# First 3x3 convolution filtered along rows and columns, its chunks in turns with the second's

## The chip, the cores and the metric

The kernel is one program on one core of a Trainium2 chip. The metric is the device time of one execution in microseconds; lower is better. Everything is float32.

## The reference, cut to what matters

The input x has shape (4, 256, 56, 56). Four layers follow each other, each of the form x = x + layer(groupnorm(x)): an involution, a block of two 3x3 convolutions, a second involution, and a channel and spatial gate. The change touches the second layer alone:

```
def layer1(x, w1, g1, b1, rm1, rv1, w2, g2, b2, rm2, rv2):
    h = relu(bn(conv3x3(x, w1), g1, b1, rm1, rv1))     # 256 -> 256 channels, padding 1
    h = bn(conv3x3(h, w2), g2, b2, rm2, rv2)
    return relu(x + h)

x = x + layer1(groupnorm(x), ...)                      # 32 groups of 8 channels
```

bn in evaluation mode is a scale and a shift for each channel. Group norm is folded into a scale `rstd` and a shift for each channel, from statistics that the layer before gathers.

## The kernel before

TensorE is called PE here, VectorE DVE, ScalarE ACT, GpSimd POOL. Channels lie on the 128 partitions, in NB = 2 blocks of 128. `conv_layer` runs between two calls of `involution_layer`, and each of the three opens its own memory pools, so that the next stage's tiles can be written only when the last users of the old ones are done. Images pass between stages through DRAM.

**Filtering along rows.** Both convolutions use the minimal filtering algorithm F(4,3) along image rows: four output columns come from six products instead of twelve. A row of 56 columns is cut into WT = 14 tiles of four. `input1` splits a normalised chunk of rows on ACT into four phases (column modulo 4, tile `ph1`, L937), and `transform` combines the phases on DVE into the six inputs `v[:, k]` (twelve instructions, L905 to L916). `weights` makes six transformed weights `u` from three taps, also on DVE (L871 to L876), after three DMAs for each input block from the ACT queue (L866 to L868). `products` does, for each of two output blocks `co` and each position k, six matmuls that add up in one PSUM bank: two input blocks and three row taps dy, the tap being a shift by whole rows in `v` (L962). One bank holds up to 20 rows x 14 tiles = 280 columns. ACT and DVE then read the six banks and combine them to four output phases (L974 to L985).

**Chunks.** The first convolution's rows are cut as C1_ROWS = (0, 20), (20, 38), (38, 56), the second's as C2_ROWS = (0, 16), (16, 36), (36, 56). For each of the four images the three chunks of the first convolution run, then the three of the second. `conv1` writes its outputs by ACT into `ph2` (L994), which holds the whole image in phases; `conv2` reads the residual input from DRAM, normalises it on ACT (L1011), adds the products (L1017), rectifies and adds in one DVE instruction (L1020), takes statistics (L1023) and stores by a DMA from the POOL queue (L1024). The transform of the next chunk is written ahead of the products of the current one, so that PE does not wait for it. The program order in this layer is left to the scheduler.

**PSUM.** Six banks are for products (`mm`), two for the small matmuls of the group norm (`gn`). In a group-norm step a mean over each group of 8 channels is a matmul with `gavg_sb` (L188, L199).

**Other lines that the prediction names.** In the involutions, L408 is a matmul of a bottleneck whose last piece has 112 columns; L498 is a DVE instruction that reads PSUM and an SBUF tile; L503 is a two-input POOL addition; L505 is a DVE instruction with two SBUF inputs; L651 is one of the two-input POOL operations of the gate.

Of the kernel before, what the change touches and what calls it, by code (L numbers as in the profile page):

```python
# [16 lines left out]
P = 128  # L17
# [54 lines left out]
def net_kernel(  # L72
# [762 lines left out]

    def conv_layer(xin, xout):
        with ExitStack() as es:
            wpool = es.enter_context(tc.tile_pool(name="cw", bufs=1))
            work = es.enter_context(tc.tile_pool(name="cwork", bufs=2))
            mm_ps = es.enter_context(tc.tile_pool(name="cmm_ps", bufs=6, space=PSUM))  # L840
            gn_ps = es.enter_context(tc.tile_pool(name="cgn_ps", bufs=2, space=PSUM))

            def one_bank():
                return gn_ps.tile([P, 512], F32, name="gn")


            xb_of = {}

            def load(b):
                xb_of[b] = work.tile([P, NB, HW], F32, name="xb", bufs=1)  # L850
                y0 = 0
                for _, y1 in C1_ROWS:
                    y1 = min(H, y1 + 1)
                    for cb in range(NB):
                        nc.sync.dma_start(xb_of[b][:, cb, y0 * W : y1 * W], xin[b][cb][:, y0 * W : y1 * W])
                    y0 = y1


            u_sb = [wpool.tile([P, NB, 3, WPOS, C], F32, name=f"u{i}_sb") for i in range(2)]

            def weights(i):
                u, wc = u_sb[i], (wc1, wc2)[i]
                for ci in range(NB):
                    w = wc[ci * P : (ci + 1) * P].rearrange("c (y x) n -> c y x n", y=3)
                    w1 = work.tile([P, 3, C], F32, name="w1")
                    nc.scalar.dma_start(u[:, ci, :, 0, :], w[:, :, 0, :])  # L866
                    nc.scalar.dma_start(u[:, ci, :, 5, :], w[:, :, 2, :])
                    nc.scalar.dma_start(w1, w[:, :, 1, :])  # L868
                    w0, w2 = u[:, ci, :, 0, :], u[:, ci, :, 5, :]
                    u1, u2, u3, u4 = (u[:, ci, :, k, :] for k in range(1, 5))  # L870
                    nc.vector.tensor_tensor(u2, w0, w2, ALU.add)  # L871
                    nc.vector.tensor_tensor(u1, u2, w1, ALU.add)  # L872
                    nc.vector.tensor_tensor(u2, u2, w1, ALU.subtract)
                    nc.vector.scalar_tensor_tensor(u4, w2, 4.0, w0, ALU.mult, ALU.add)
                    nc.vector.scalar_tensor_tensor(u3, w1, 2.0, u4, ALU.mult, ALU.add)
                    nc.vector.scalar_tensor_tensor(u4, w1, -2.0, u4, ALU.mult, ALU.add)  # L876
# [12 lines left out]
            norm_of = {}  # L889

            def norm(b):
                rstd, shift = norms[1][b]

                shift2 = small.tile([P, NB], F32, name="shift2")
                nc.vector.tensor_add(shift2, shift, bn["t2"])
                norm_of[b] = rstd, shift, shift2

            def transform(v, ci, ph, n):

                d = [ph[:, j, :, :WT] for j in range(4)] + [ph[:, j, :, 1:] for j in range(2)]  # L900
                vs = [v[:, k, ci, : n * WT].rearrange("p (r t) -> p r t", t=WT) for k in range(WPOS)]
                tmp = [work.tile([P, CV_ROWS + 2, WT], F32, name=f"d{k}", bufs=1) for k in range(3)]
                a, c, e = (t[:, :n] for t in tmp)
                tt, stt = nc.vector.tensor_tensor, nc.vector.scalar_tensor_tensor
                stt(a, d[2], -4.0, d[4], ALU.mult, ALU.add)  # L905
                stt(c, d[1], -4.0, d[3], ALU.mult, ALU.add)
                tt(vs[1], a, c, ALU.add)
                tt(vs[2], a, c, ALU.subtract)
                tt(c, d[4], d[2], ALU.subtract)
                tt(e, d[3], d[1], ALU.subtract)  # L910
# [120 lines left out]
            for b in range(B):  # L1031
                for i in range(3):
                    nv = input1(b, i + 1) if i < 2 else None
                    if i == 2:
                        nv = input2(0)
# [87 lines left out]
```

## Time and profile before

| | us |
|---|---|
| median of 3 runs | 1947.86 |
| lowest and highest | 1942.15, 1957.1 |
| the profiled execution, its own time | 1955.35 |
| span of its profile | 1953.6 |
| first involution, up to its last matmul's follow-up | 0 to 539 |
| convolution matmuls, first start to last end | 555.6 to 1323.2 |
| second involution and gate | 1323.2 to 1953.6 |

The slices of the page show the three stages (each digit is the busy share of a slice of 48.8 us in tenths):

```
PE   5899999999869999999999999997999899999876
DVE  4685767856678686668657865854766666666773
ACT  2345445444343122312331232113655555555532
POOL 2233432334300000000000000000000581580672
```

The profile names an instruction by its line of the kernel, its engine, its operation and the tiles it writes and reads. In a group of instructions the numbers after the bar are the busy time in us, the mean ns of one, and the idle time before them. A matmul's recorded length includes its way through the array, so neighbours overlap; the pace of a row of them is the busy time over the count. The same holds, less strongly, for DVE, whose next instruction starts some 0.08 us before the recorded end of the last if it does not need its result.

### The profile page before, as it was taken

The numbers are of one execution on the slowest core, as the hardware profiler recorded it, in microseconds if no ns is written. First come the engines' busy times: TensorE is split into PE (matmuls) and PEld (weight loads), VectorE is DVE, ScalarE is ACT, GpSimd is POOL, SyncE is SP. The second block draws the span as 40 slices with busy tenths as digits, with TensorE's granted clock in tenths as the row PEclk, the third lists the DMA queues.
The fourth block names the chain that finished last, engine by engine and source line by source line (L and its number), as shares of the span: only waits on it lengthen the run. The fifth ranks groups of instructions, "written<-read, shape, count | busy, mean of one in ns | idle before, by whom it ended". The sixth has DMA issues, their size and how long they took to land.

```text
span 1953.6 us, 55107 instructions
## 1 busy us (share of the span) xinstructions
PE 1801.3 (92%) x23766; PEld 1555.4 (80%) x23766; DVE 1322.8 (68%) x2843; ACT 766.1 (39%) x1672; POOL 433.1 (22%) x631
## 2 busy tenths in 40 slices
PE   5899999999869999999999999997999899999876
PEld 4888879878748987898789888984887777877765
DVE  4685767856678686668657865854766666666773
ACT  2345445444343122312331232113655555555532
POOL 2233432334300000000000000000000581580672
PEclk9999999999979999999999999998999999999995
DMA  3444534444251011101111110113533763763651
GB/s 100 149 148 150 165 107 137 150 130 146 88 206 66 22 67 45 67 32 56 45 67 43 57 34 1 43 47 128 161 130 128 222 175 135 222 188 103 180 151 72
DMA packets 66962, 213.19 MB, mean 109 GB/s; under 512 B 13660, under 2 KB 21648, under 8 KB 63392
## 3 DMA queue, kind: packets, MB, share of 16 engines
q1 hardware_dynamic: 44526, 137.45, 22.5%
q0 software_dynamic: 14848, 65.85, 10.3%
q10 hardware_dynamic: 7346, 6.38, 1.1%
q8 instruction: 187, 3.06, 0.7%
q14 instruction: 55, 0.45, 0.1%
HBM read 73.76 MB, written 49.16 MB: 63 GB/s over the span
## 4 chain that ended last, share of the span: by engine, by line
PE 75%; DVE 13%; DMA 5%; POOL 3%; issue 2%; ACT 1%; SPq 0%; ACTq 0%; POOLq 0%; DVEq 0%
PE mm L962 39%; PE ps L478 16%; DVE kt L454 9%; PE ps L436 8%; PE ps L408 5%; PE ps L364 4%; DVE un L498 1%; PE ps L665 1%; DMA xw<-xw 1%; DMA gx<-x 1%; PE ps L561 1%; DMA w<-in_wc_dram 1%; DMA xs<-in_x_dram 1%; DVE st L807 0%; POOL norm_sb L130 0%
## 5 line engine op out<-in xcount | busy, mean ns | idle before, releaser
L962 PE MATMUL mm<-v,u_sb 128*128 128x280 f32 (+2 forms) x3456 | 766.7, 384 | 19.4 <-DVE u_sb L872 19.4
L962 PEld LDWEIGHTS mm<-v,u_sb 128*128 128x128 f32 x3456 | 653.9, 190 | 126.9 <-issue 19.4
L478 PE MATMUL ps<-kt,xw 126*32 126x48 f32 (+1 forms) x12544 | 382.8, 236 | 46.6 <-issue 23.8
L478 PEld LDWEIGHTS ps<-kt,xw 126*32 126x32 f32 (+1 forms) x12544 | 341.5, 122 | 97.9 <-issue 56.3
L454 DVE TENSOR_TENSOR kt<-ps,zb_sb 126x798 f32<-126x798 f32 x384 | 357.6, 979 | 57.6 <-PE ps L436 56.8
L436 PE MATMUL ps<-hp,z_sb 64*126 64x133 f32 x6144 | 384.1, 280 | 11.0 <-DVE kt L454 6.4
L436 PEld LDWEIGHTS ps<-hp,z_sb 64*126 64x126 f32 x6144 | 366.3, 187 | 25.8 <-DVE kt L454 7.7
L447 ACT ACTIVATE kt<-ps,zb_sb 126x133 f32<-126x133 f32 x768 | 224.6, 442 | 167.5 <-PE ps L436 167.5
L498 DVE SCALAR_TENSOR_TENSOR un<-ps,s,un 128x240 f32<-128x240 f32 x224 | 102.5, 457 | 130.4 <-ACT un L493 126.4
L498 DVE SCALAR_TENSOR_TENSOR un<-ps,par_sb,un 128x240 f32<-128x240 f32 x224 | 98.5, 457 | 122.1 <-ACT un L491 117.9
L1024 POOL DMA_DIRECT2D x<-xr x24 | 13.1, 548 | 560.7 <-DVE xr L1020 515.1
L503 POOL TENSOR_TENSOR xs<-un,xs 128x240 f32<-128x240 f32 x112 | 72.3, 666 | 224.1 <-DVE un L498 224.1
L365 ACT COPY xw<-ps 126x896 f32<-126x896 f32 x112 | 101.6, 907 | 51.0 <-PE ps L364 43.6
L364 PE MATMUL ps<-ident_sb,strip_sb 128*126 128x128 f32 x784 | 112.9, 285 | 2.2 <-ACT un L493 1.3
L408 PE MATMUL ps<-xs,redn 128*128 128x504 f32 (+1 forms) x224 | 98.0, 585 | 9.4 <-DMA xs<-x 7.4
L937 ACT ACTIVATE ph<-xb,norm_sb 128x294 f32<-128x294 f32 (+2 forms) x96 | 80.7, 897 | 64.4 <-DVE d L913 35.9
L493 ACT ACTIVATE un<-ps,bn_t,s 128x240 f32<-128x240 f32 x112 | 60.3, 539 | 116.3 <-PE ps L478 108.5
L491 ACT ACTIVATE un<-ps,par_sb 128x240 f32<-128x240 f32 x112 | 50.3, 449 | 130.3 <-PE ps L478 128.5
L994 ACT ACTIVATE ph<-y,bn_t,bn_s 128x252 f32<-128x252 f32 (+1 forms) x96 | 54.8, 600 | 109.2 <-DVE y L984 73.9
L364 PEld LDWEIGHTS ps<-ident_sb,strip_sb 128*126 128x126 f32 x784 | 85.8, 143 | 11.8 <-ACT un L493 1.4
L130 POOL TENSOR_TENSOR norm_sb<-norm_sb,mhalf 128x1 f32<-128x1 f32 x32 | 18.9, 589 | 338.0 <-DVE norm_sb L129 331.5
L978 DVE SCALAR_TENSOR_TENSOR y<-mm,y 128x280 f32<-128x280 f32 (+2 forms) x48 | 20.5, 427 | 103.2 <-PE mm L962 103.2
(144 smaller groups left out, 1583.3 us busy)
## 6 DMA issues: line engine op xcount, KB each, us to landing
xw<-xw SPq DMA_DIRECT2D x168, 252.0 KB
xw<-xw SPq DMA_DIRECT2D x224, 126.0 KB
xw<-xw POOLq DMA_DIRECT2D x56, 252.0 KB, 4.5
x<-xs POOLq DMA_DIRECT2D x8, 1568.0 KB, 7.7
xs<-in_x_dram SPq DMA_DIRECT2D x6, 1568.0 KB
xs<-x SPq DMA_DIRECT2D x6, 1568.0 KB
x<-xs SPq DMA_DIRECT2D x6, 1568.0 KB
gx<-x POOLq DMA_DIRECT2D x42, 224.0 KB, 5.4
```

Source lines behind the costliest of these rows:

```text
L364: nc.tensor.transpose(ps[:Q, k * P : (k + 1) * P], flat[:, k * Q : (k + 1) * Q], ident_sb)
L365: nc.scalar.copy(xw[:, :NSB, :], ps[:Q, : NSB * P].rearrange("q (n c) -> q n c", n=NSB))
L408: nc.tensor.matmul(ps[:, : rows * W], redn[:, ci].rearrange("p i r -> p (i r)"), xs_of[b, ci][:, j * ROWS_H * W : (j * ROWS_H + rows) * W] ...
L436: nc.tensor.matmul(ps[:Q, i, k * NT : (k + 1) * NT], z_sb[i * R : (i + 1) * R, cb * GB // 2 + gp, z0 : z0 + Q], hp[i * R : (i + 1) * R, py ...
L447: nc.scalar.activation(kt[:, g0 + i, pb, :, k], ps[:Q, i, k * NT : (k + 1) * NT], AF.Identity, bias=zb_sb[:, cb * GB + g0 + i, p0 + k : p0 ...
L454: nc.vector.tensor_tensor(kt[:, g0 : g0 + 2, pb], ps[:Q, :, : PB * NT].rearrange("q i (k t) -> q i t k", k=PB), zb_sb[:, cb * GB + g0 : cb ...
L478: nc.tensor.matmul(v[m * j : m * j + m, i, :, k * TP : (k + 1) * TP], xw[:, window(ty), m * j : m * j + m], kt[:, ng * j : ng * j + ng, :, ...
L493: nc.scalar.activation(part, o[0], AF.Identity, bias=bn["t4"][:, cb : cb + 1], scale=bn["s4"][ng][:, 0, cb : cb + 1])
L498: nc.vector.scalar_tensor_tensor(part, o[e], s, part, ALU.mult, ALU.add)
L503: nc.gpsimd.tensor_tensor(dst, u, dst, ALU.add)
L937: nc.scalar.activation(ph1[:, q, r0 : r0 + hi - lo, t0 : t0 + WT], xr[:, j], AF.Identity, bias=shift[:, ci : ci + 1], scale=rstd[:, ci : c ...
L962: nc.tensor.matmul(ps[:, : n * WT], u[:, ci, dy, k, co * P : (co + 1) * P], v[:, k, ci, dy * WT : (dy + n) * WT], start=(i == 0), stop=(i ...
```

## The change

The first convolution is filtered along both directions: F(4,3) along rows as before and F(2,3) along columns of the image. Two output rows then come from four products over a pair of rows instead of six row taps. The second convolution stays filtered along rows only. Around it the whole layer is written anew:

- `u1_sb` has four row entries y in place of three. `row_weights` makes the row filtering of the weights in steps; `column_weights` then sums them over the taps, for two positions k at a time, on POOL for positions (1, 2) and (0, 5) and on DVE for (3, 4). The factors 1/2 of F(2,3) are in the combination, and part of the factors of F(4,3) goes into the scales (`s1_6`, `scales`).
- `columns` builds the four column inputs of one position from `v` by four POOL instructions of 280 or 252 elements, in two tiles `v2` (five buffers). Positions 1 and 2 are built in the step before, the others inside the step.
- `conv1` does, for each position k, four groups of four matmuls (two output blocks side by side in a bank, two input blocks added), each over half of the chunk's rows: 140 or 126 columns. It reads four banks for each position: one ACT copy, two DVE additions, and two DVE instructions that finish the row pair. A chunk's outputs are combined over both blocks at once, in instructions of 560 or 504 elements, three of them on POOL. Their last part is a `tail` that runs in the next step.
- `conv2` combines its banks as they come. The residual is added before the rectification, scaled so that ACT's scale by `rstd` brings it back; ACT rectifies into `res`, and POOL adds `res` to the input and stores it (`finish`).
- In `transform` the first differences for positions 0 and 5 go to POOL, two of twelve instructions.
- The chunks run in the order conv1(0), conv1(1), conv2(0), conv1(2), conv2(1) and so on over all images, ending with conv2(11). Loads are by chunk and block, with one or two rows read twice.
- All eight PSUM banks form one pool.
- Into each step's twelve places `after[0..11]` the pieces of other chunks' work are put by lists written by hand, and `in_order` then pins every engine to the program order in the layer, from the first matmuls on.

The diff, cut to its core:

```diff
-            mm_ps = es.enter_context(tc.tile_pool(name="cmm_ps", bufs=6, space=PSUM))
-            gn_ps = es.enter_context(tc.tile_pool(name="cgn_ps", bufs=2, space=PSUM))
+            mm_ps = es.enter_context(tc.tile_pool(name="cmm_ps", bufs=8, space=PSUM))
...
+            tt, stt = nc.vector.tensor_tensor, nc.vector.scalar_tensor_tensor
+            ptt = nc.gpsimd.tensor_tensor
...
+            def column_weights(ci, ks, eng, scratch):
+                at = slice(ks[0], ks[1] + 1, ks[1] - ks[0])
+                w0, w1, w2, w3_ = (u1_sb[:, ci, y, at, :] for y in range(4))
+                s = y_tile(scratch)[:, : 2 * C].rearrange("p (k n) -> p k n", k=2)
+                eng.tensor_tensor(s, w0, w2, ALU.add)
+                eng.tensor_tensor(w3_, s, w1, ALU.subtract)
+                eng.tensor_tensor(w1, s, w1, ALU.add)
...
             def transform(v, ci, ph, n):
...
+                ptt(vs[0], d[0], d[2], ALU.subtract)
+                ptt(vs[5], d[5], d[3], ALU.subtract)
...
-                tt(a, d[0], d[2], ALU.subtract)
-                stt(vs[0], c, 0.25, a, ALU.mult, ALU.add)
-                tt(a, d[5], d[3], ALU.subtract)
-                stt(vs[5], e, -4.0, a, ALU.mult, ALU.add)
+                stt(vs[0], c, 0.25, vs[0], ALU.mult, ALU.add)
+                stt(vs[5], e, -4.0, vs[5], ALU.mult, ALU.add)
...
+            def columns(i, k):
...
+                for pair in (((1, 2, ALU.add), (2, 1, ALU.subtract)), ((0, 2, ALU.subtract), (1, 3, ALU.subtract))):
+                    t = work.tile([P, 2 * NB, CV_ROWS // 2 * WT], F32, name="v2", bufs=5)
+                    v2_of.setdefault((i, k), []).append(t)
+                    for e, (p, q, op) in enumerate(pair):
+                        o = t[:, e * NB : (e + 1) * NB, : m * WT].rearrange("p c (r t) -> p c r t", t=WT)
+                        ptt(o, d[p], d[q], op)
+
+            KS = (1, 2, 3, 4, 0, 5)
...
+            def conv1(i, after, tail):
...
+                for s, k in enumerate(KS):
+                    (va, vb) = v2_of[i, k]
+                    banks = []
+                    for v2, e, y in ((va, 0, 1), (va, 1, 3), (vb, 0, 0), (vb, 1, 2)):
+                        ps = one_bank()
+                        banks.append(ps[:, : NB * m])
+                        for co in range(NB):
+                            for ci in range(NB):
+                                nc.tensor.matmul(
+                                    ps[:, co * m : (co + 1) * m],
+                                    u1_sb[:, ci, y, k, co * P : (co + 1) * P],
+                                    v2[:, e * NB + ci, :m],
+                                    start=(ci == 0),
+                                    stop=(ci == NB - 1),
+                                )
+                    m1, m2, m0, m3 = banks
+                    h = work.tile([P, NB * CV_ROWS // 2 * WT], F32, name="h")[:, : NB * m]
+                    nc.scalar.copy(h, m1)
...
+                    tt(o[:, 0], by_row_(h), by_row_(m2), ALU.add)
+                    tt(h, h, m2, ALU.subtract)
+                    run_all(after[2 * s])
+                    stt(o[:, 0], o[:, 0], 0.5, by_row_(m0), ALU.mult, ALU.add)
+                    stt(o[:, 1], by_row_(h), 0.5, by_row_(m3), ALU.mult, ALU.subtract)
+                    if s + 2 < WPOS:
+                        columns(i, KS[s + 2])
+                    if s == 1:
+                        ptt(a, mi[1], mi[2], ALU.add)
+                    if s == 2:
+                        tt(mi[1], mi[2], mi[1], ALU.subtract)
+                    if s == 3:
+                        ptt(b, mi[3], mi[4], ALU.add)
+                    if s == 4:
+                        tt(mi[3], mi[3], mi[4], ALU.subtract)
+                        stt(mi[0], a, -1.0 / 6, mi[0], ALU.mult, ALU.add)
+                        stt(mi[0], b, 1.0 / 24, mi[0], ALU.mult, ALU.add)
+                        ptt(b, b, a, ALU.subtract)
+                    run_all(after[2 * s + 1])
...
+            def conv2(i, after, sums, tail):
...
+                    def residual(y, j, x=xj, co=co):
+                        s = sc[:, 2 if j in (1, 2) else 1, co : co + 1]
+                        y = y.rearrange("p (r t) -> p r t", t=WT)
+                        stt(y, y, s, x[:, j], ALU.mult, ALU.add)
...
+                        else:
+                            yd = part("yd", co)
+                            stt(yd, q, 1.0 / 6, ps, ALU.mult, ALU.add)
+                            stt(yd, t, 1.0 / 3, yd, ALU.mult, ALU.add)
+                            residual(yd, 3)
+                            rectified(yd, 3)
+                            stt(t, t, 0.5, q, ALU.mult, ALU.add)
+                            residual(t, 1)
+                            rectified(t, 1)
+                        run_all(after[WPOS * co + s])
+
+                    def finish(x=x, res=res, co=co):
+                        ptt(x, x, res, ALU.add)
+                        nc.gpsimd.dma_start(xout[bb][co][:, y0 * W : y1 * W], x)
...
+            order = [(1, 0)]
+            for i in range(1, n_chunks):
+                order += [(1, i), (2, i - 1)]
+            order.append((2, n_chunks - 1))
...
+                if conv == 1:
+                    run_all(tail1)
+                    if tail2:
+                        after[0].append(tail2.pop(0))
+                    if nxt is not None and nxt[0] == 2:
+                        j = nxt[1]
+                        place(after, input2(j, 0), (0, 0, 0, 1, 1, 2, 2, 3, 3, 4, 4))
+                        place(after, input2(j, 1), (4, 5, 5, 5, 6, 6, 7, 7, 8, 8, 9))
...
+                    if nxt is not None and nxt[0] == 1:
+                        j = nxt[1]
+                        place(after, input1(j, 0), (1, 2, 2, 2, 3, 3, 3, 3, 3, 4, 4))
+                        place(after, phases(j, 1), (4, 4, 5, 5, 5))
...
+                        place(after, input1(j, 1), (6, 6, 6, 7, 7, 7, 8, 8, 8, 9, 9))
+                        for k in range(2):
+                            after[9 + k].append(lambda j=j, k=k: columns(j, KS[k]))
...
+            in_order(since)
```

In the changed kernel the matmuls of `conv1` are line 1043 and those of `conv2` line 1138, the column inputs line 1019, and the four DVE drains of a position lines 1055 to 1059.

## The prediction

> **What bounds the kernel now.** I read the page's engine row and slices, the chain that ended last, the busy times of the convolution stage, and then the instruction groups by shape.
>
> ```profile
> PE 1801.3 (92%) x23766; PEld 1555.4 (80%) x23766; DVE 1322.8 (68%) x2843; ACT 766.1 (39%) x1672; POOL 433.1 (22%) x631
> ```
>
> ```profile
> 555.60:1323.20 767.60, 767.60 (x3480) 656.91 (x3481) 548.66 (x1340) 195.47 (x308) 19.20 (x44) 1.00 0.14 49
> ```
>
> ```profile
> 555.59 192.83 PE mm L962 x864
> ```
>
> The first line is the page's engine row. The second is the stretch from the first to the last convolution matmul; its columns are length, then busy time of PE, PEld, DVE, ACT, POOL, then the granted clock. PE is busy in all 767.6 us; DVE in 548.7 (71%), POOL in 19. The third line is the chain: one image is a single run of L962 without a wait. So this stage is bound by PE, and what shortens PE shortens it, until another engine takes over.
>
> ```profile
> L962 PE MATMUL mm<-v,u_sb 128*128 128x280 f32 x1728 | 413.6, 400 | 19.4 <-DVE u_sb L872 19.4
> L962 PE MATMUL mm<-v,u_sb 128*128 128x252 f32 x1152 | 245.5, 375 | 0.0
> L408 PE MATMUL ps<-xs,redn 128*128 128x112 f32 x32 | 4.8, 271 | 0.0
> ```
>
> ```profile
> L651 POOL TENSOR_TENSOR gn<-gn,sfb 128x448 f32<-128x448 f32 x42 | 48.7, 1159 | 0.0
> L503 POOL TENSOR_TENSOR xs<-un,xs 128x240 f32<-128x240 f32 x56 | 39.2, 700 | 223.3 <-DVE un L498 223.3
> ```
>
> Busy time over count gives the pace of a matmul record: 0.239 us at 280 columns, 0.213 at 252. A float32 matmul leaves two records (3456 for 1728 in the code). The L408 line has 8 runs of 4 records, each with new weights: (4.8/8 - 0.271)/3 = 0.110 us a record. The POOL lines give 2.2 ns per element and 0.17 us per instruction for two inputs.
>
> ```profile
> 551.78 0.47 DVE L905 SCALAR_TENSOR_TENSOR d<-ph 128x308 f32<-128x308 f32 x1
> 552.17 0.47 DVE L906 SCALAR_TENSOR_TENSOR d<-ph 128x308 f32<-128x308 f32 x1
> ```
>
> ```profile
> 1318.31 0.45 DVE L979 SCALAR_TENSOR_TENSOR y<-mm,y 128x280 f32<-128x280 f32 x1
> 1318.79 0.45 DVE L982 SCALAR_TENSOR_TENSOR y<-y,y 128x280 f32<-128x280 f32 x1
> ```
>
> ```profile
> 1521.43 1.14 POOL L651 TENSOR_TENSOR gn<-gn,sfb 128x448 f32<-128x448 f32 x1
> ```
>
> ```profile
> 1521.86 0.97 DVE L505 SCALAR_TENSOR_TENSOR xs<-un,xs 128x240 f32<-128x240 f32 x1
> ```
>
> From the starts: an independent DVE instruction takes 0.39 us at 308 elements (1.04 ns each plus 0.07); one that needs its predecessor takes 0.48 at 280, so 0.12 more. The last two lines: POOL reads SBUF until 1522.57; DVE L505, which has two SBUF inputs and is 0.41 long in its median, starts inside that time and ends at 1522.83, one plain pass of 240 elements after POOL.
>
> **What the Trainium skill says.** "SBUF — State Buffer", section Who interferes with whom: a DVE instruction with two SBUF inputs and a GpSimd instruction that reads SBUF exclude each other for their whole length; one with at most one SBUF input is left alone. The trace agrees: L505 above, while L498 (PSUM and SBUF inputs) shows 0.47 beside the same POOL work. "TensorE: Matmul & The Clock Gate", section LDWEIGHTS, makes a weight load as long as its columns, 128/1.2 = 107 ns; the 0.110 us at 112 columns fits. "GPSIMD Engine Reference", section 3.1, puts a two-input elementwise operation at about 2.6 cycles per element; 2.2 ns here.
>
> **The change, part by part.**
>
> *PE.* A first-convolution chunk now has 6 x 4 x 2 x 2 = 96 matmuls of half its rows where it had 144/2 = 72 of all rows. Before: 576 records x 0.239 + 1152 x 0.213 = 383 us. After: 768 records at 140 columns and 1536 at 126. The column slope, (0.239 - 0.213)/28, brings 140 columns to about 0.118; at 126 the slope gives 0.10, but the weight load holds it at 0.110. Sum 91 + 169 = 260. PE's need falls by 123 us to 645. Bounds on a record at 126: 0.10 and, were the recorded load length of 0.19 the pace, 0.19.
>
> *DVE, own time* (12 chunks of each convolution, elements from the shapes): first-convolution drains, 288 instructions, 75.3k elements, 133 dependent: 78 + 20 + 16 = 114. Combinations of 504 or 560 elements, 84: 59. Second convolution from PSUM, 144: 56; from SBUF, 96: 39. Residuals, 96, one input with stride 4: 45 if the stride is free, 71 if it costs what L1017 (strided in and out, 0.64 at 280) costs; I take 57. Input transforms, 480 (ten a piece; two went to POOL): 188. Statistics 112 x 0.30 = 34. Norms and the second filter's weights 21. Sum 568 us; two instructions moved to POOL and the saved finishing pass pay for most of what the column sums add. 568 is under PE's 645, but 88% of it.
>
> *POOL.* 288 column instructions x 0.75 = 216; 96 transform parts x 0.80 = 77; 36 combinations x 1.32 = 48; 24 finishing adds x 2.47 = 59; 24 DMA issues x 0.55 = 13. Sum 413 us, from 19. Of it 2.2 ns x 146.6k elements = 322 us hold the read port.
>
> *The port.* 756 DVE instructions (transforms, combinations, residuals, SBUF sums) have two SBUF inputs: 253 us. 322 + 253 = 575, so the port is taken 89% of PE's 645 us. No trace of before shows this mix. Bounds on the DVE time lost: nothing, if POOL always falls on drains from PSUM; 322 us, as DVE works in order and each POOL hold stops at most one of its instructions. Mean hold 0.73 us. About six in ten DVE instructions have two SBUF inputs, so right behind one the next waits the whole hold with chance 0.6 (0.44 us), and behind a PSUM drain POOL's hold is over or nearly so; I take 0.39 us per POOL instruction where DVE is pressed, less a quarter for the time in which DVE waits for PE anyway: 0.29 x 444 = 130 us. DVE then needs 568 + 130 = 698, over PE's 645: it becomes the bound. Add 22 us in which it cannot work (the first drain, half of the last second-convolution chunk of 34 us): stage 720.
>
> *Order.* In a first-convolution step POOL has 16 column instructions, 4 transform parts, 3 combinations and the finishing add: about 22 us for PE's 21 to 23. The finishing add heads POOL's queue there: it waits for the last five DVE instructions and a rectification (2.9 + 0.7 us after the matmuls), holds the queue 3 us, and only behind it come the columns of the third position, wanted 7.2 us in. Worked through, the columns land near 10 us and again late at the fifth position: PE waits some 5 us per step, which is not added, since DVE, not PE, sets the pace then. In the second-convolution steps PE's 27 to 34 us cover all else.
>
> *Ends.* First matmul: before, it waited for weights (DMA to 554.3, DVE 0.97). Now, after the DMAs, POOL has in its queue 5 filter sums for positions 0 and 5 and 6 for positions 1 and 2 (512 elements, 1.3 us each), four transform parts of 0.85 and two columns of 0.8: 19 us from about 549, plus some 5 of port waits against 12 DVE weight sums, so near 573 for 555.6: +17 (bounds +10, +25). Last chunk: the finishing add on POOL (2.5) and a rectification (0.65) stand where DVE's L1020 (1.3) stood: +3. The loads on SP and ACT keep their size but for rows read twice; at a DMA share of 14% they cost nothing.
>
> Sum: 720 + 17 + 3 - 767.6 = -28 us on the profiled 1955.35: 1927. That execution stands 0.4% above the median 1947.86, so 1920.
>
> **The rivals.**
> 1. PE stays the bound: the holds fall on drains, DVE loses under 77 us. DVE has 645 - 568 = 77 us of room. For it: 432 DVE drains from PSUM and 112 statistics, 204 us, can lie beside POOL's holds. Against: transforms and columns are laid in the same steps. 645 + 20 - 767.6 = -103: 1845.
> 2. Slower: DVE and POOL stop each other nearly every time. In the first-convolution steps both have over 21 us of own work for PE's 22, and transforms come in runs of two or three, each waiting a whole column hold. It decides from 0.40 us per POOL instruction (178 us lost: 568 + 178 + 22 = 768; with the ends it is slower already from 0.36). At 0.5: 222 + 568 + 22 + 20 = 832, +64: 2010. Against: the drains between, and POOL's own waits, which give DVE the port.
> 3. The matmuls don't shrink as said: a weight load paces a record at its recorded 0.19 us. 2304 x 0.19 = 438, PE 823, + 20: +75, about 2020. Against: L408's 0.110.
>
> **How the numbers follow.** A run of a kernel like this tells about 1% from no change. Forecast 0.48 (1900 to 1945 for 0.24 to 0.35 us a POOL instruction), rival 1 0.12, rival 2 0.34, rival 3 0.06. Faster by over 1% (under 1928): rival 1 and two thirds of the forecast, 0.45. Within 1%: the rest of the forecast and the near edge of rival 2, 0.20. Slower 0.35. The range 1860 to 2015 leaves out the outer parts of rivals 1 and 2 and rival 3. Both signs hold much of the chance; the forecast's own range is 1900 to 1945.
>
> **What would show it.** In the profile after: L1043 records at 0.11 to 0.12 us in a run; DVE busy above 90% of the stage and its two-input instructions lengthened beside POOL while the drains L1055 to L1059 are not; PE idle in first-convolution steps, released by POOL's L1019 or by DVE; first matmul near 573. I am wrong if PE is busy throughout, if the transforms keep their 0.47 us, or if the stage is over 768 us.

## The result, and the profile after

The changed kernel takes 2060.0 us (median of 4 runs, 2057.7 to 2062.9) against 1946.2 for the kernel before in the same measurement: ratio 1.0576, interval 1.053 to 1.0622. It is slower by 5.8%. The profiled execution took 2057.68 us, its span 2055.9. These are the lines that answer to those shown of before: the page's engine row, the stretch from the first to the last convolution matmul, and the groups.

```profile
PE 1737.3 (85%) x24342; PEld 1532.9 (75%) x24342; DVE 1592.5 (77%) x2890; ACT 814.8 (40%) x1768; POOL 868.1 (42%) x1071
```

```profile
574.60:1437.20 862.60, 708.56 (x4056) 638.04 (x4056) 789.25 (x1363) 236.51 (x395) 427.07 (x468) 0.91 0.13 44
```

```profile
L1043 PE MATMUL mm<-v,u_sb 128*128 128x126 f32 (+1 forms) x2304 | 314.0, 301 | 164.5 <-POOL v L1019 125.3
...
L1019 POOL TENSOR_TENSOR v<-v 128x252 f32<-128x252 f32 (+1 forms) x288 | 219.3, 794 | 0.2
...
L1183 POOL TENSOR_TENSOR xr<-xr,res 128x1120 f32<-128x1120 f32 (+1 forms) x24 | 57.5, 2398 | 128.9 <-ACT res L1125 128.9
...
L973 DVE TENSOR_TENSOR v<-d,d 128x308 f32<-128x308 f32 (+2 forms) x48 | 106.8, 2224 | 0.8
```

PE's work did fall, but the stage went from 767.6 to 862.6 us. PE is idle 154 us of it, DVE is busy in 789 of 863, and the granted clock is 0.91 where it was 1.00. The last line is the one to stop at: L973 adds two tiles of 308 elements, which takes 0.47 us alone, and its mean is 2.22 us. Where before had one unbroken run of L962 in the chain of work that ended last, the chain is now mostly DVE's; these pieces of it (start, length, what) stand around one step from the second convolution to the first:

```profile
752.97 0.40 DVE v L975
753.39 5.99 DVE d L977
759.38 0.40 DVE d L979
...
770.84 0.45 DVE h L1056
771.34 1.63 issue
...
774.15 6.92 DVE v L973
```

Outside the stage: the first matmul starts 19 us later (574.6 for 555.6), and what follows the last matmul is 11.7 us shorter (618.7 for 630.4). Together with the stage's 95 that is the 102 us between the two profiled executions. The medians lie 114 us apart.

### Two kinds of waits

The timeline of the changed kernel at the first of the two long pieces, DVE and POOL:

```profile
752.93 0.56 POOL L1184 DMA_DIRECT2D x<-xr  x1 [0.30 <-POOL xr L1183]
753.39 5.99 DVE L977 TENSOR_TENSOR d<-ph 128x308 f32<-128x308 f32 x1
```

```profile
773.01 0.57 POOL L1184 DMA_DIRECT2D x<-xr  x1 [0.30 <-POOL xr L1183]
773.60 0.86 POOL L964 TENSOR_TENSOR v<-ph 128x308 f32<-128x308 f32 x1
774.07 7.00 DVE L973 TENSOR_TENSOR v<-d,d 128x308 f32<-128x308 f32 x1
774.41 0.85 POOL L965 TENSOR_TENSOR v<-ph 128x308 f32<-128x308 f32 x1
775.22 5.52 POOL L1019 TENSOR_TENSOR v<-v 128x280 f32<-128x280 f32 x8
775.92 10.45 PE L1043 MATMUL mm<-v,u_sb 128*128 128x140 f32 x64 [7.29 <-POOL v L1019]
```

The second one is L973: it stands through ten POOL instructions in a row (two transform parts, eight columns) and ends when the burst ends. There are 17 such stops in the stage, seven of L977 over eight POOL instructions and ten of L973 over ten, 5.6 to 7.0 us each. A DMA issue on POOL, the store of `finish`, ends half a microsecond or less before each of them. The stage has 23 such issues. All 17 with POOL work ready behind them have a long stop, and the six with nothing behind them for 3 us or more have none. Where no DMA issue stands ahead, the engines take turns. Some 13 us later in the same step:

```profile
787.23 7.23 POOL L1019 TENSOR_TENSOR v<-v 128x280 f32<-128x280 f32 x8
787.52 0.93 DVE L987 SCALAR_TENSOR_TENSOR v<-d,v 128x308 f32<-128x308 f32 x1
...
789.09 1.25 DVE L1065 TENSOR_TENSOR y<-y,y 128x560 f32<-128x560 f32 x1
...
790.26 1.07 DVE L969 SCALAR_TENSOR_TENSOR d<-ph 128x308 f32<-128x308 f32 x1
791.25 0.94 DVE L971 SCALAR_TENSOR_TENSOR d<-ph 128x308 f32<-128x308 f32 x1
```

Eight columns of the same size take 7.23 us instead of 5.52, and each two-input DVE instruction waits for about one of them. From here on "lost time" is DVE's time above what the shortest twentieth of the same line and shape takes, summed over the instructions of 200 elements or more in the stage: 219 us here, of which 126 in waits over 1.2 us. The drains L1055 (one SBUF input, the other in PSUM) show no loss: 0.41 us at 252 elements with POOL beside them all the time (31 of them) and without (17).

The page "SBUF — State Buffer" of the Trainium skill, section SBUF: two separate sides, says that of a DVE instruction with two SBUF inputs and a POOL instruction that reads SBUF, whichever starts first has the shared ports for the whole instruction and the other is blocked. The last timeline agrees: each wait is about one POOL instruction. A stop over ten of them, as in the second timeline, goes further than the hold of one instruction, and the experiments look for what brings it. The prediction's "left alone" is narrower on that page (section Who interferes with whom): it holds outside the two-port modes of VectorE. The drains above, at 0.41 us with POOL and without, are left alone.

### The profile page after: what moved, and what is told of

Read it like the earlier page. It is cut to its first block, busy times and chain, and to the rows that moved or that the text cites. A ratio compares the mean times of both kernels' runs of the same rounds, so it can differ in the third digit from the quotient of the medians.

```text
span 2055.9 us, 57328 instructions
## 1 busy us (share of the span) xinstructions
PE 1737.3 (85%) x24342; PEld 1532.9 (75%) x24342; DVE 1592.5 (77%) x2890; ACT 814.8 (40%) x1768; POOL 868.1 (42%) x1071
## 4 chain that ended last, share of the span: by engine, by line
DVE 45%; PE 37%; issue 7%; DMA 4%; POOL 3%; ACT 3%; SPq 1%; ACTq 0%; POOLq 0%; DVEq 0%
PE ps L478 14%; DVE kt L454 9%; PE ps L436 8%; PE ps L408 4%; DVE v L973 4%; PE mm L1138 4%; PE ps L364 4%; DVE y L1122 3%; DVE d L977 3%; DVE d L971 2%; DVE h L1056 1%; DVE un L498 1%; DVE v L983 1%; DVE y L1055 1%; DVE st L1189 1%
## 5 line engine op out<-in xcount | busy, mean ns | idle before, releaser
L1043 PE MATMUL mm<-v,u_sb 128*128 128x126 f32 (+1 forms) x2304 | 314.0, 301 | 164.5 <-POOL v L1019 125.3
L1043 PEld LDWEIGHTS mm<-v,u_sb 128*128 128x128 f32 x2304 | 302.7, 211 | 176.1 <-POOL v L1019 142.0
L1138 PE MATMUL mm<-v,u_sb 128*128 128x280 f32 (+1 forms) x1728 | 396.0, 390 | 7.2 <-DVE u_sb L876 7.2
L1138 PEld LDWEIGHTS mm<-v,u_sb 128*128 128x128 f32 x1728 | 332.6, 194 | 63.4 <-issue 5.4
L1019 POOL TENSOR_TENSOR v<-v 128x252 f32<-128x252 f32 (+1 forms) x288 | 219.3, 794 | 0.2
L1125 ACT ACTIVATE res<-y,cscale,norm_sb 128x280 f32<-128x280 f32 (+1 forms) x96 | 82.5, 859 | 252.0 <-DVE y L1122 251.0
L1052 ACT COPY h<-mm 128x252 f32<-128x252 f32 (+1 forms) x72 | 26.3, 380 | 240.2 <-PE mm L1043 137.6
L964 POOL TENSOR_TENSOR v<-ph 128x308 f32<-128x308 f32 (+2 forms) x48 | 45.6, 949 | 174.5 <-ACT ph L951 170.7
L1183 POOL TENSOR_TENSOR xr<-xr,res 128x1120 f32<-128x1120 f32 (+1 forms) x24 | 57.5, 2398 | 128.9 <-ACT res L1125 128.9
L973 DVE TENSOR_TENSOR v<-d,d 128x308 f32<-128x308 f32 (+2 forms) x48 | 106.8, 2224 | 0.8
```

The source lines that it names most:

```text
L1019: ptt(o, d[p], d[q], op)
L1043: nc.tensor.matmul(ps[:, co * m : (co + 1) * m], u1_sb[:, ci, y, k, co * P : (co + 1) * P], v2[:, e * NB + ci, :m], start=(ci == 0), stop= ...
L1125: nc.scalar.activation(rj[:, j], y.rearrange("p (r t) -> p r t", t=WT), AF.Relu, bias=sc[:, 0, co : co + 1], scale=rstd[:, co : co + 1],)
L1138: nc.tensor.matmul(ps, u2_sb[:, ci, dy, k, co * P : (co + 1) * P], v[:, k, ci, dy * WT : dy * WT + m], start=(j == 0), stop=(j == NB * 3 - 1),
```

## The experiments

A burst is a row of POOL instructions with no pause between them. A slot is one of a step's twelve places `after[0..11]`. Theory A: the DMA issue on POOL lets the burst behind it through without DVE getting a turn. Theory B: taking turns at the port costs this much whatever stands on the queue. Theory C: POOL's order, columns behind `finish`, makes PE wait. Theory D: DVE's own work sets the pace. The ratio to before is given with its interval. Where an expectation speaks of 384 column instructions, it should say 288 (6 positions, 4 instructions, 12 chunks), and its 192 and 256 of them are 144 and 192. The runs lie on several chips, each measured beside the kernel before, so close kernels are compared by their ratios.

| kernel | us | ratio to before | stage | DVE busy (lost) |
|---|---|---|---|---|
| changed | 2060.0 | 1.0576 (1.053-1.0622) | 862.6 | 789 (219) |
| e1 store on SP | 2005.2 | 1.0278 (1.0254-1.0303) | 810.4 | 735 (161) |
| e3 finish in slot 3 | 2061.8 | 1.0576 (1.0548-1.0603) | 866.7 | 792 (224) |
| e2 columns on DVE | 2040.0 | 1.0466 (1.0434-1.0498) | 842.1 | 757 (106) |
| e4 no columns | 1924.4 | 0.987 (0.9834-0.9906) | 736.6 | 663 (103) |
| e5 small DMAs | 2069.4 | 1.0603 (1.0583-1.0623) | 869.9 | 794 (217) |
| e6 store later on POOL | 2027.8 | 1.0397 (1.0371-1.0423) | 829.9 | 753 (183) |
| e7 e1 and e3 | 2011.9 | 1.0309 (1.0287-1.0332) | 818.4 | 736 (174) |
| e8 three banks | 2014.1 | 1.0332 (1.0305-1.0358) | 819.9 | 687 (160) |
| e9 half the columns on DVE | 2007.7 | 1.0298 (1.0235-1.0361) | 816.5 | 708 (157) |
| e10 columns as copies | 1954.7 | 1.0001 (0.9976-1.0026) | 761.9 | 678 (113) |
| e11 rows only | 1975.2 | 1.0108 (1.0063-1.0154) | 794.3 | 560 (102) |
| e12 first two filtered | 1961.6 | 1.0049 (1.0029-1.0069) | 766.2 | 615 (126) |
| e14 last two filtered | 1929.8 | 0.9891 (0.9864-0.9919) | 743.9 | 617 (124) |
| e15 last four filtered | 1945.1 | 0.9964 (0.9944-0.9985) | 763.0 | 695 (155) |

### e1: the store on another queue

```
-                        nc.gpsimd.dma_start(xout[bb][co][:, y0 * W : y1 * W], x)
+                        nc.sync.dma_start(xout[bb][co][:, y0 * W : y1 * W], x)
```

> The store of the residual chunk is issued from SP's queue in place of GpSimd's; nothing else changes. Theory A (the long stops of VectorE, 17 of 5.6 to 7.0 us in the trace of the changed kernel, come from the DMA issue that stands on GpSimd just before its burst of column instructions): these 17 stops shrink to one GpSimd instruction each, under 1.2 us; VectorE's lost time falls from 219 us to some 120, and the time from 2060 to 1950-1990. Theory B (VectorE and GpSimd exclude each other whatever stands on the queue): the long stops stay behind GpSimd's addition, 2030-2060. Theory C (GpSimd's own order, the columns behind the addition): no change but the 0.57 us of each issue, 2040-2060.

All 17 long stops are gone; no DVE instruction waits for more than two POOL instructions. A mere pause of POOL ahead of a burst does not bring one: in e1 POOL pauses for 0.5 to 8.8 us ahead of some twenty bursts, and no instruction is stopped through any of them. The instruction that stood 5.99 us, L977 of the same step, now takes turns (timeline of e1):

```profile
747.94 7.08 POOL L1019 TENSOR_TENSOR v<-v 128x280 f32<-128x280 f32 x8 [0.48 <-DVE v L973]
748.22 0.82 DVE L977 TENSOR_TENSOR d<-ph 128x308 f32<-128x308 f32 x1
748.96 0.94 DVE L979 TENSOR_TENSOR d<-ph 128x308 f32<-128x308 f32 x1
749.93 0.96 DVE L981 SCALAR_TENSOR_TENSOR v<-d,d 128x308 f32<-128x308 f32 x1
750.81 1.07 DVE L983 SCALAR_TENSOR_TENSOR v<-d,d 128x308 f32<-128x308 f32 x1
```

The time falls by 55 us. That is less than theory A alone expected (to 1950-1990), and lost time is 161 us where some 120 were expected: the waits over 1.2 us fell from 126 to 28, but the short ones rose from 93 to 133, since instructions that no longer stand through a burst now meet it one by one.

### e3 and e7: POOL's order

```
-                        after[0].append(tail2.pop(0))
+                        after[3].append(tail2.pop(0))
```

> The closing addition of a chunk and its store go from slot 0 of the next first-convolution step to slot 3, so GpSimd comes to the columns without waiting for ScalarE's last rectified row. Theory C (the columns of the third row position are late because they stand behind the addition, which waits for conv2's end): PE's wait of about 7.3 us at the third group of each such step goes for 8 steps, about 60 us, time near 2000. Theory A (DMA issue): the long stops move to whatever stands behind the store, the time stays within 2030-2070. Theory B: the same, 2030-2070.

> Both edits: the store on SP's queue and the addition in slot 3 in place of slot 0. With the long stops gone, theory C gets its second test: if the columns are late because they stand behind the addition on GpSimd, PE's waits for them fall by some 3 us in each of 11 steps and the time from 2005 to 1965-1985. If VectorE's whole load (574 us of its own and 161 lost, 735 of 810) sets the stage, the order on GpSimd is worth little: 1995-2010.

In e3 PE's waits for the columns fall from 125 to 83 us, as theory C wants, and the time does not move (2062). The long stops moved with the store: ten-instruction stops now fall on L1065 and on L977, 16 of them. (Nearly all L1065 of each shape are stopped there, so e3's lost time is taken from the shortest of each line and shape; by that measure the changed kernel has 223.) In e7, without long stops, moving `finish` takes the same waits from 114 to 85 us, and the time is not the expected 20 to 40 us shorter: the ratios are 1.0309 and 1.0278, with intervals that overlap. PE is idle for 113 us of the stage in both. What PE no longer waits for at one place it waits for at others. Theory C falls.

### e6 and e5: the DMA issue, moved and multiplied

e6 leaves the store on POOL but issues that of the second half in slot 8, behind the last columns; e5 takes e1 and puts a DMA of four bytes per partition ahead of each group of four column instructions inside a first-convolution step.

```
+                        after[8].append(tail2.pop())          # e6: the store alone
```

```
+                        nc.gpsimd.dma_start(tiny[s % 4], s1_6[:, 0:1])     # e5
                         columns(i, KS[s + 2])
```

> The store stays on GpSimd's queue, but the one of the chunk's second half is issued in slot 8 of the first-convolution step, behind the last columns, while the addition stays at the head. Theory A (DMA issue straight ahead of a burst): the ten stops over ten GpSimd instructions vanish or shrink to the few instructions that follow slot 8; those of the other half (seven over eight instructions, which slot 6 of the second convolution's step causes) stay. Time about halfway between 2060 and 2005: 2020-2040. Theory B (the addition ahead of the burst, a long holder of 2.55 us, is what lets the burst through): ten long stops stay, time 2050-2065.

> On the kernel with the store on SP, a DMA of 4 bytes per partition is issued on GpSimd's queue ahead of each group of four column instructions inside a first-convolution step, 48 in all; they serve nothing else. Theory A (a DMA issue on GpSimd lets the instructions behind it through without VectorE getting a turn): stops of VectorE across four or more GpSimd instructions come back, 25 to 48 of them, 2.2 to 2.6 us each, none of 5.6 to 7.0; time 10 to 40 us above the 2005 of the store on SP. Theory B (the long stops came from the store's size, 448 KB of traffic, or from the addition ahead of it): no stop over two GpSimd instructions, time within 2000-2020 for the 48 issues of some 0.57 us.

e6: the ten stops over ten instructions are gone, the seven over eight, whose store was not moved, are there. 2028 lies between 2060 and 2005, as expected of theory A. The addition L1183 still heads the burst in each of the ten places, so it isn't the addition. And e6 issues as many DMAs from POOL as the changed kernel, so its gain isn't the time of the issues. e5: 24 stops over four to six POOL instructions (25 to 48 were expected) and 19 over three are back, none was in e1, and the time is 2069, 64 us above e1. One of them:

```profile
780.27 0.55 POOL L1062 DMA_DIRECT2D tiny<-s  x1
780.64 3.77 DVE L975 TENSOR_TENSOR v<-d,d 128x308 f32<-128x308 f32 x1
780.85 2.77 POOL L1019 TENSOR_TENSOR v<-v 128x280 f32<-128x280 f32 x4
```

So it is the issue itself, of a whole store or of four bytes per partition, ahead of POOL work that is ready. Why the issue does this the trace does not show. The 64 us are more than the 10 to 40 expected. DVE's lost time rose by 56 us. Beside it each of the 48 issues holds POOL's queue for 0.55 us (26 us), and PE's waits for columns rose from 114 to 133 us; what each of these adds is not shown.

### e4, e10, e2: what is left, the columns

```
-                                    v2[:, e * NB + ci, :m],
+                                    d[p][:, ci],              # e4: columns() returns at once
```

```
-                        ptt(o, d[p], d[q], op)
+                        nc.gpsimd.tensor_copy(o, d[p])        # e10, on e1
+                        tt(o, d[p], d[q], op)                 # e2, on the changed kernel
```

> The column combinations are left out: the first convolution's matmuls read the row-transformed input itself, so the output isn't the reference's; matmuls and drains are as many as before. Theories A and B: GpSimd falls by 216 us, the stops of VectorE with it: lost time under 60 us and the stage near PE's 660-700, time 1860-1910. Theory D (VectorE's own work and the order of drains set the pace, with the stops not decisive): the stage stays above 780, time above 1980.

> On the kernel with the store on SP, each column combination on GpSimd is replaced by a copy of its first operand, so GpSimd's order, count and buffers stay and only the second input is left out (the output isn't the reference's). If the remaining loss is the turn taking between two-input instructions of the two engines: VectorE's lost time falls from 161 to about 100 us, as without columns at all, first-convolution steps to 25-29 us, time 1935-1965 with the columns' own GpSimd time still there. If it is GpSimd's own time in order: 1985-2005.

> All column additions run on VectorE in place of GpSimd. GpSimd's work falls from 427 to some 210 us in the stage, VectorE gets 384 two-input instructions of about 0.33 us more at 280 elements, some 125 us of its own time (570 to 695). Theory B and my prediction's wait per GpSimd instruction: lost time falls to some 60 us at most, the sum is 695 + 60 + idle, stage 780-830, time 1980-2030. Theory C (order on GpSimd): PE's wait for columns goes over to VectorE, which is as late with its drains: 2000-2060.

The stretch of the stage in e1, e10 and e4, one line each:

```profile
574.55:1385.00 810.45, 697.44 (x4056) 632.08 (x4056) 735.24 (x1363) 236.90 (x395) 441.50 (x445) 0.92 0.14 47
```

```profile
572.69:1334.56 761.87, 686.90 (x4056) 624.14 (x4056) 678.28 (x1363) 235.74 (x395) 345.71 (x445) 0.95 0.14 50
```

```profile
562.41:1299.05 736.64, 679.15 (x4056) 608.84 (x4056) 662.49 (x1377) 241.08 (x400) 220.61 (x186) 0.97 0.16 53
```

From e1 to e10 the columns keep their count and place, and each is shorter by the second input (0.59 for 0.93 us in the mean at 280 elements, beside DVE). DVE's lost time falls by 48 us, the stage by 49, the time by 50, within the 1935-1965 expected of the turn taking. A copy still stops a two-input DVE instruction, but for less: L975 at 308 elements takes 0.66 to 0.69 us beside copies in e10, 0.81 to 0.93 beside additions in e1, 0.47 alone. e10 shortens POOL's own time and the port's hold together, so it doesn't tell these two apart. Without any columns (e4, which keeps the store on POOL, but with no burst behind it) another 25 us of the stage go, and the first matmul comes 10 us earlier. Its 1924 is far below the 1980 from which theory D would hold, so DVE's own work with its drains does not set the pace by itself. It misses the 1860-1910 of theories A and B too, since 103 us are still lost where under 60 were expected. In e2 the lost time halves, but DVE's own work grows by 81 us; PE waits 153 us for columns, now for DVE's. That is better than the changed kernel by 20 us and worse than e1. 2040 lies outside theory B's range for this run and inside theory C's; against C stand e3 and e7, which move POOL's order alone.

### e8 and e9: relieving DVE or POOL

e8 folds the factor 1/2 into the weights and lets the matmuls add m0 and m3 to m2, so that two drains remain of four; e9 also gives the second pair of columns to DVE. Both have the store on SP.

```
-for v2, e, y in ((va, 0, 1), (va, 1, 3), (vb, 0, 0), (vb, 1, 2)):
+for terms in (((va, 0, 1),), ((va, 1, 3), (vb, 0, 0)), ((va, 1, 3), (vb, 1, 2))):
```

```
-                        ptt(o, d[p], d[q], op)
+                        (tt if pair[0][0] == 0 else ptt)(o, d[p], d[q], op)
```

> On the kernel with the store on SP: the factor 1/2 of the column filter goes into the weights (two more ScalarE instructions for each of the six weight calls) and the sums m2+m0 and m2+m3 are accumulated by the matmuls, 20 in place of 16 per position. PE gets 576 records more (288 matmuls of two records, some 65 us at 0.113), VectorE 144 of its 288 drains less (62 us at 0.43). If VectorE's load sets the stage: first-convolution steps fall from 28-34 us to 26-29, time 1950-1975. If PE and its waits for columns set it: 2005-2060.

> On the kernel with three banks per position and the store on SP, the second pair of column combinations of each position (192 instructions of the 384) goes to VectorE, which has 133 us idle there. If GpSimd's chain of columns (some 0.8 us each beside VectorE) is what PE waits for in the first-convolution steps: these fall from 30-36 us to 28-31, time 1965-1990. If VectorE's turns set them: 2000-2025.

DVE's busy time fell by 49 us in e8, PE's rose by 51 with the added matmuls, and the time rose by 9. That is in the range given for PE and its waits for columns; but e8 takes from one engine what it gives to another, so it doesn't tell which of the two loads set the step before. In e9 POOL's busy time fell by 136 us more. The time is 6 us lower, with intervals that overlap, in the range given for VectorE's turns, yet DVE's lost time hardly moved (157 for 160). So taking work off POOL gained little here. What holds e8's and e9's first-convolution steps at 29 to 37 us, with PE busy in 27 to 32 of them, stays open.

### e11 to e15: how much filter pays

With the store on SP, unfiltered positions run on rows as in the second convolution, their banks copied by ScalarE.

```
+                    if s < FILTERED:      # e11: 0, e12: 2; e14, e15: if s >= ROWS_ONLY, 4 and 2
...
+                    else:
+                                    nc.tensor.matmul(ps, u1_sb[:, ci, dy, k, co * P : (co + 1) * P],
+                                        v[:, k, ci, dy * WT : (dy + n) * WT], start=(j == 0), stop=(j == NB * 3 - 1))
+                            nc.scalar.copy(mi[k][:, co * n * WT : (co + 1) * n * WT], ps)
...
-                            place(after, g, [4 + co, 5 + co, 6 + co, 7 + co, 8 + co, 9 + co])
+                            place(after, g, [2, 5 + co, 6 + co, 9 + co, 10 + co, 10 + co])   # e14, e15
```

> The turns, the pinned orders and the work given to GpSimd and ScalarE without the column filter: the first convolution runs on rows as it did before (12 matmuls of 252 or 280 columns for each position), ScalarE copies its banks, the store is on SP. PE's need in the stage is again some 768 us; VectorE's is 574 less the 288 drains of 0.43, 450. If the rest of the change costs nothing: first matmul near 555, stage 768 to 780, time 1935-1960. If the turns or the pinned orders carry a loss of their own (VectorE and GpSimd in each other's way without any columns): stage above 800, time above 1970.

> As the kernel with the store on SP, but only the first two of the six positions are filtered along the columns, the two whose columns are made inside the second convolution's step; the other four run on rows, with ScalarE copying their banks. PE's need falls by a third of the 123 us that the filter saves, 768 to 727; GpSimd loses 256 of 384 column instructions, VectorE 192 of its 288 drains (574 to 490 us of its own). If the loss comes from the columns inside the first convolution's steps: PE bounds, stage 730-750, time 1900-1930, under both kernels. If the filter loses wherever its columns stand: 1960-2000.

> The last two positions of each chunk are filtered along the columns and the first four run on rows, so no filtered weight stands ahead of the first matmul, and the steps of the norms between two images stand three slots apart. If the prologue's 19 us and the norms' waits of some 20 us were what kept two filtered positions at 1961: first matmul near 556, PE waits in the stage under 20 us, time 1920-1940. If the filter's gain is lost elsewhere: 1945-1965.

> The same with the last four positions filtered; two of the four get their columns inside the first convolution's step. PE's need falls by another 41 us to 686. If PE still bounds: 1890-1910. If columns inside the step bring the turns between VectorE and GpSimd back: 1935-1965.

e11 has no columns at all, and still takes 1.1% more than before: its stage is 27 us longer than before's. 18 of them are waits of PE, 3.5 in the first chunk and the rest for the norms of an image, whose steps now stand inside second-convolution steps (L188 and L199, 1.9 to 3.3 us each); PE's busy time is 8 us longer. So part of the loss comes with the new order and not with the filter. e12 gains PE time but keeps the late start (574.9). e14 filters the last two positions of each chunk, so that their weights are made behind the others', and spreads the norms' steps. Its stretch and its longest waits of PE (total, times, longest; the 24.9 us are the wait ahead of the first matmul):

```profile
562.06:1306.01 743.95, 733.66 (x3672) 638.46 (x3672) 616.53 (x1179) 254.44 (x449) 287.75 (x256) 0.99 0.15 53
```

```profile
PE mm L1069 <- DVE v L973: 28.4, 2, 24.9
PE mm L1158 <- DVE u_sb L876: 4.0, 2, 3.3
PE mm L199 <- DVE d L196: 2.8, 3, 0.9
```

PE is busy in 734 of 744 us at a clock of 0.99. At 1929.8 us e14 is faster than before by 1.1% (interval 0.8 to 1.4) and the fastest of the kernels that leave nothing out. Its stage is 24 us shorter than before's and starts 6.5 us later, at 562.1 and not near the 556 expected. Without any filter the same spread of the norms was not run; had e11 waited for its norms as little as e14 (3 us for 15), it would still be some 30 us slower than e14, as an estimate. With four positions filtered (e15) PE needs less, 713 us, but DVE is busy 695 of 763 and PE waits again: 1945. In these runs the best amount of filter is what DVE and POOL carry while PE still bounds.

## Why the prediction was wrong, point by point

*Held.* The matmuls' price: within a run, neighbouring L1043 records start 0.112 us apart in the middle at 126 columns and 0.119 at 140, so rival 3 is out. The 0.118 at 140 was luck in part: the slope that I named, (0.239 - 0.213)/28, gives 0.109 there. DVE's own time: 789 less 219 is 570, I had 568. POOL: 427 for 413. The first matmul: 574.6 for 573. The strided residual L1122 takes 0.727 us at 280 elements with no POOL beside it, the upper of my two bounds. The drains are not lengthened, the transforms are.

*Failed first: the wait per POOL instruction.* I took 0.29 us by 444, 130 us. It was 219 us, 0.49 apiece, which is rival 2's sum of 222. The reasoning "right behind one the next waits the whole hold with chance 0.6" had every wait end with one POOL instruction. For most instructions it did: of some 200 in the changed kernel that lost more than 0.06 us, all but 18 waited for one at the most. But 17 stood through eight or ten, and those 17 account for some 100 us. A DMA issue ahead of the burst was not in the reasoning at all. e1 takes the store off POOL and only then comes near the price: 161 us over 445 POOL instructions, 0.36. That rival 2's sum fits is luck: its reason was that nearly every instruction waits a whole column's hold, and without the stops behind the DMA issue that gave 0.36 and not 0.5.

*Failed second: the idle time and with it the bound.* I added 22 us to DVE's total; DVE was idle 73 us. With the higher price it is why even e1 takes 2005 and not 1920: 0.36 for 0.29 makes 31 us, an idle time of 75 for 22 another 53. It is also why rival 2's 2010 was too low for 2060. I compared totals of the whole stage. The steps have different bounds: a steady second-convolution step is 34.0 us long and PE is busy for 34.0 of it, DVE for 30.7; a first-convolution step is 31 to 41 long, PE busy for 24 to 28, DVE for 30 to 39. What DVE has over in the one kind doesn't serve the other. Of the 73 us, 55 lie in second-convolution steps (18 of them in the last pair), 18 in the others. The bound is the sum over steps of the slowest engine, not the slowest engine's sum.

*Not counted: PE's clock.* I held PE's need at 645 us; its busy time was 708. After an idle stretch the matmuls run slower. Windows of the changed kernel around the 7.3 us wait (the last three numbers are granted clock, DMA share, GB/s):

```profile
756.70:766.00 9.30, 7.32 (x57) 6.74 (x55) 9.12 (x17) 1.26 (x2) 2.34 (x4) 1.00 0.01 2
766.00:776.00 10.00, 1.74 (x9) 1.44 (x9) 8.69 (x14) 2.78 (x5) 5.51 (x6) 0.58 0.34 116
776.00:780.00 4.00, 4.00 (x17) 4.00 (x18) 4.00 (x1) 0.39 (x1) 4.00 (x7) 0.50 0.00 0
780.00:786.50 6.50, 6.38 (x49) 6.17 (x47) 6.43 (x12) 1.99 (x3) 3.37 (x4) 0.91 0.00 0
```

In the first 4 us after the wait 17 records start, 0.235 us each, at half clock. The 0.91 of the next 6.5 us leaves another 1.2 us at half clock; then the pace is back. The page "TensorE: Matmul & The Clock Gate", Part 1, says that an idle window of about 3.4 us halves the clock and one as long of work restores it; the trace agrees in the main, with some 5 us of work here before the clock was back. So this wait of PE cost some 2.6 us more than its length. Over the stage 95 us of PE's busy time lie at half clock, which makes some 47 of the 63 us above 645. DVE's drains of these matmuls come later by as much; what that adds to the stage no run shows apart.

*Order.* "PE waits some 5 us per step, which is not added": PE waited 87 us for columns beyond the first wait of 38.6, 8 us in each of 11 steps. That it needn't be added was right in a sense: e7 took 29 us of these waits away and the time did not fall.

*The sum.* Stage 720 + 89 (waits) + 51 (idle) + 2 (own time) = 862; ends +19 and -11.7 where I had +17 and +3. Of the 112 us (ratio 1.0576) that the change cost, the runs show, taken away in this order and by the ratios' differences times 1950: the store's issue on POOL 58, the columns' second input 54, the columns' remaining work with part of the prologue 26. Without these three the change would gain 25 us (e4, 0.987), though PE's need fell by 123: there PE is busy 679 of the stage's 737 us and DVE 663. In a steady second-convolution step PE is busy for all 34.0 us; in a steady first-convolution step, 22 to 27 us long, both engines are busy but for some 2 us at most. The rest goes in the first steps (105 us in all, PE busy for 82) and in waits for the norms.

The 11.7 us at the end have no shown cause, and most likely they are no effect of the change. The +3 itself held: the first L408 matmul of the second involution starts 16.6 us after the last convolution matmul, before 13.6. From there the code is the same, yet in the 15 profiles with the new layer what follows the last convolution matmul takes 612 to 630 us (630.4 in e12), so single executions scatter by more than the 11.7. The profiled execution of before stands 7.5 us above its median, that of the changed kernel 2.3 below, which together could be most of the 11.7. From 177 to 377 us after the last convolution matmul the granted clock was 0.98 for 0.95 before.

## What to carry to other kernels

Put no DMA issue on GpSimd's queue ahead of GpSimd work that shares VectorE's port; another queue cost one word and gave half of the loss back. When work is moved from a bound engine to others, make the sum step by step with each step's own slowest engine, and price each wait of PE with the slow clock behind it. A saving that can be dosed should be dosed: a third of this filter beat the whole of it, the new layer without it, and the kernel before.

## What the runs showed of the hardware that was not expected

- Behind a DMA issue on GpSimd a waiting two-input VectorE instruction lost its turn for the whole burst that followed: 8 or 10 instructions, 5.6 to 7.0 us; 3 to 6 instructions behind a DMA of four bytes per partition. Without the issue (e1) it waited for one, at most two.
- A one-input GpSimd copy stops two-input VectorE instructions too (0.66 to 0.69 for 0.47 us), for less than an addition does (0.81 to 0.93).
- PE's clock was at half for some 3 to 6 us after each of its waits of 6.3 to 7.6 us in the changed kernel's stage, and the mean clock of the stage went with PE's idle time: 0.91 with 154 us idle, 0.97 with 57 (e4), 0.99 with 10 (e14).
- A VectorE input with a stride of four elements cost 0.73 us at 280 elements against 0.45 with unit stride (L1168). The strided instruction (L1122) also reads a factor for each partition, which L1168 does not, so the two are not told apart.
